# A ring of row blocks for xT, zeroed edge blocks in A, and output stores tile by tile on the sync queue

## The chip, the cores and the metric

The kernel runs on one core of a Trainium2 chip. The metric is device time in microseconds (us); "time" below is that of one whole execution. A profiled execution is described by its span, from the first instruction to the last, and by its own device time, which is a little longer.

## The reference

The input x has 4 images of 256 channels, 64 by 64, in float32. Two layers follow each other.

```python
# layer 0: attention over 49 dilated neighbours, the weights of which are computed from x
k = conv(x, w1 (128,256,7,7), dilation 2, padding 6) + b1
k = conv(k, w2 (49,128,1,1)) + b2
attn = softmax(k, axis=1)                       # 49 shares at each pixel
xp = pad(x, 6)                                  # zeros around the image
shifts = [xp[:, :, 2u:2u+64, 2v:2v+64] for u in 0..6, v in 0..6]
x = einsum('bkchw,bkhw->bchw', shifts, attn)    # each pixel: weighted sum of 49 neighbours
# layer 1: residual bottleneck, batch norm with the batch's own moments
h = relu(bn(conv1x1(x, 256->64)))
h = relu(bn(conv3x3(h, 64->64)))
h = bn(conv1x1(h, 64->256))
return relu(h + x)
```

## The kernel before, in words

Since the dilation is 2, pixels of even and odd rows and columns never mix. The image is therefore handled as four subimages (q = 0 to 3) of 32 by 32 pixels for each of four images: 16 units (b, q), the order of which is in `units`.

**Layer 0, the shares (to about 500 us).** The 7x7 convolution is done along rows by a short-convolution transform on VectorE and along columns by matmuls into eight PSUM banks (`column_convs`, L263), once for each transform point and half of the channels. Then `exponents` and `shares` make the softmax. `shares` writes the 49 shares of a pixel into wide zero-padded rows (`pads`), and `turn` (L556) transposes these rows on TensorE, so that they become `amat`: for each group g of images, column pair c and block m of rows, a matrix A that holds for every output pixel its shares, laid out over the 128 input pixels (4 rows of 32) that it can reach. ScalarE (L574) and VectorE (L572) copy A from PSUM.

**Layer 0, the sum (about 503 to 661 us).** `gather(n, half)` (L728) multiplies, for unit n and half of the channels, tiles of xT (pixels on partitions, channels along the row) by A. There are two xT tiles per unit, c = 0 and c = 1. Tile c = 0 holds the rows of the subimage shifted by 3, c = 1 by 1. A tile has NT + 1 = 9 blocks of 128 pixels; block 0 begins and block 8 ends outside the image, and the parts outside are zeros. In each c, nine matmuls i = 0 to 8 add into one PSUM bank of 512 columns, i = 0 and i = 8 with 64 columns each, the others with 128. The stationary operand is block i of the xT tile, the moving one is A. Everything is float32; each such matmul stands in the profile as two records, each with a weight load of its own.

The tiles for unit n + 2 are brought by `more_xt`, after the gathers of unit n have been issued: `load_xt` (L109) zeroes blocks 0 and 8 on GpSimd (L113, L114) and loads tile c = 0 by three DMAs on the sync queue (L115 the first rows, L116 the main body, L120 the last rows); `shift_xt` (L122) makes tile c = 1 from tile c = 0, its lower 64 partitions by a copy on ScalarE (L124), its upper 64 by a copy on GpSimd (L125) and a memset of the last block (L126). There are two pairs of tiles, so that unit n + 2 uses the pair of unit n. All of them lie in one large tile, `outer`.

`keep_y` copies the sums from PSUM, on VectorE for half 0 (L768) and on ScalarE for half 1 (L766), and stores them to DRAM on the sync queue (L769). After every second unit `conv1` (L780) does the first 1x1 convolution of a finished pair of units and gathers statistics (L788).

**Layer 1.** The first batch norm follows the last `conv1` (L850 to L911). The 3x3 convolution is done partly directly (L947), partly by a transform (L959). The moments of the third convolution's result are worked out from h itself (L1020, L1024) and then in small steps at L1040 to L1053. Finally, for each of 16 output tiles of 128 channels by 2048 pixels, four times: a matmul (`conv3`, L1007), a fused multiply-add of the residual on VectorE (L1065), and a relu on ScalarE (L1069) into one of four tiles `ops`. Each tile is stored by a DMA of 1 MB, issued on ScalarE's queue (L1073).

**What sets the order.** In the blocks `manual_schedule(...)` the order on the named engines is the order of the code. The softmax and `turn` part, up to `more_xt(1)`, is such a block for VectorE, TensorE, ScalarE and the sync queue, not for GpSimd. The gather loop (L799 to L815) and all that follows are in none: there the framework orders each engine's queue when the program is built. [...]

Of the kernel before, what the change touches and what calls it, by code (L numbers as in the profile page):

```python
# [43 lines left out]
AF = mybir.ActivationFunctionType  # L44
ALU = mybir.AluOpType
# [3 lines left out]
P = 128  # L49
B, C, H, W = 4, 256, 64, 64  # L50
# [5 lines left out]
MID = 64  # L56
# [37 lines left out]
def conv_seq_kernel(ctx: ExitStack, tc: tile.TileContext, xp, xt, w1, b1, w2t, b2, m1t, g1, be1,  # L94
# [14 lines left out]
    def load_xt(t, b, q, c=0):  # L109

        src = xt[b].rearrange("j p q c -> (j p) q c")[:, q, :]
        r0 = 2 * c - 3
        nc.gpsimd.memset(t[:, 0, :], 0.0)  # L113
        nc.gpsimd.memset(t[:, NT, :], 0.0)  # L114
        nc.sync.dma_start(out=t[-r0 * R : P, 0, :], in_=src[: (4 + r0) * R])  # L115
        nc.sync.dma_start(  # L116
            out=t[:, 1:NT, :],
            in_=src[(4 + r0) * R : (4 * NT + r0) * R].rearrange("(a p) c -> p a c", p=P),
        )
        nc.sync.dma_start(out=t[: -r0 * R, NT, :], in_=src[(4 * NT + r0) * R :])  # L120

    def shift_xt(t, x):  # L122

        nc.scalar.copy(t[:MID], x[MID:])  # L124
        nc.gpsimd.tensor_copy(t[MID:, :NT], x[:MID, 1:])  # L125
        nc.gpsimd.memset(t[MID:, NT], 0.0)  # L126

# [9 lines left out]
    ut = arena[:, UT:].rearrange("p (h n v) -> p h n v", h=NH, v=KV)  # L139

    amat = arena[:, :AT].rearrange("p (g x c m e) -> p g x c m e", g=2, x=R // 2, c=2, e=4)
    XT = (NT + 1) * C
    xts = {}

    units = [(b + 2 * g, 2 * a + c) for b in range(2) for g in range(2) for c in range(2) for a in range(2)]
# [410 lines left out]
    def turn(s, h, shared=False):  # L556

        row = pads[(2 * s + h) % 3]
        for j in range(4):
            pt = accall[:, 2 * (n_turn[0] % NS) : 2 * (n_turn[0] % NS) + 2].rearrange("p a (m n) -> p (a m) n", n=P)  # L560
            if h == 0 and s == 0:
                pt = accall[:, :2].rearrange("p a (m n) -> p (a m) n", n=P)
            n_turn[0] += 1
            for k in range(2):
                for w in range(4):
                    o = 35 - (WS * s + 4 * h + w) + P * (1 - k)
                    nc.tensor.transpose(pt[:, 4 * k + w, :], row[:, j, w, o : o + P], ident)  # L567
            for g in range(2):
                dst = amat[:, g, 2 * (2 * s + h) + j % 2, j // 2].rearrange("p (k n) e -> p k n e", k=2)
                src = pt[:, :, 64 * g : 64 * g + 64].rearrange("p (k w) n -> p k n w", k=2)  # L570
                if shared and g:
                    nc.vector.tensor_copy(dst, src)  # L572
                else:
                    nc.scalar.copy(dst, src)  # L574
# [49 lines left out]
    for n, (p, factor, left) in enumerate(passes):  # L624
# [8 lines left out]
        for s in range(NS):  # L633
# [12 lines left out]
            if p is None and 0 < s < NS - 1:  # L646
# [2 lines left out]
                exponents(s - 1)  # L649
                shares(s - 1)  # L650

    xtiles = [outer[:, i * XT : (i + 1) * XT].rearrange("p (a c) -> p a c", c=C) for i in range(4)]
# [14 lines left out]
    with tc.manual_schedule(  # L669
        engines={mybir.EngineType.DVE, mybir.EngineType.PE, mybir.EngineType.Activation, mybir.EngineType.SP}  # L670
    ):
        turn(0, 1)
        load_xt(xtiles[0], *units[0])
        exponents(2)
        turn(1, 0)
        exponents(3)
        shares(2)
        turn(1, 1)
        turn(2, 0)
        shares(3)  # L680
        load_xt(xtiles[1], *units[0], 1)
        turn(2, 1, True)
        turn(3, 0, True)
        turn(3, 1, True)
        xts[(*units[0], 0)], xts[(*units[0], 1)] = xtiles[:2]
        nc.scalar.preload_act_table(AF.Sqrt)
        more_xt(1)
# [35 lines left out]
    def bank(kind):  # L723

        n_bank[kind] += 1
        return accall[:, 5 * kind + n_bank[kind] % (5 - 2 * kind)]

    def gather(n, half):  # L728

        b, q = units[n]  # L730
        m = (b // 2 * Q + q) * NT
        pts = []
        for c in range(2):
            x = xts[b, q, c]
            a = amat[:, b % 2, :, c]
            pt = bank(0)
            for i in range(NT + 1):
                lo, hi = max(0, 128 * i - 64), min(1024, 128 * i + 64)
                o = 64 * max(0, i - 1)

                blocks = slice(m + i - 1, m + i + 65, 65)
                if i == 0:
                    blocks = slice(m + 64, m + 65)
                if i == NT:
                    blocks = slice(m + NT - 1, m + NT)
                nc.tensor.matmul(  # L746
                    pt[:, o : o + hi - lo],
                    x[:, i, half * P : (half + 1) * P],
                    a[:, :, blocks, :].rearrange("p x m e -> p m x e"),
                    start=(i == 0),  # L750
                    stop=(i == NT),
                    skip_group_check=True,
                )
            pts.append(pt)
        return pts

    def keep_y(n, half, pts):
# [242 lines left out]
        load_y(n)  # L1000
    sc2, sh2 = from_sums(sums2, bn12[:, 2:3], bn12[:, 3:4])

    def conv3(b, q, i, half):
        a, c = divmod(q, 2)
        part, slot, q = slice(a * MID, (a + 1) * MID), b % 2, b // 2 * 2 + c
        pt = pb_.tile([P, 512], F32, tag="pb", name="pconv3")
        nc.tensor.matmul(  # L1007
            pt, w3m[part, half * P : (half + 1) * P], h2[part, slot, q, 512 * i : 512 * (i + 1)], start=True, stop=True
        )
        return pt  # L1010


    moments = pb_.tile([P, 512], F32, tag="pb", name="moments")
# [20 lines left out]
    one = small(1)[:MID]  # L1034
    mv3 = small(NH, 2)
    sq3 = small(NH, 1)
    nc.gpsimd.memset(one, 1.0)
    for g in range(2):
        half = slice(g * MID, (g + 1) * MID)
        nc.vector.tensor_copy(prod[half], moments[half, half])  # L1040
    nc.vector.tensor_copy(sums, moments[:, P : P + 1])
    pt = pb_.tile([P, 512], F32, tag="pb", name="pprod")
    nc.tensor.matmul(pt[:MID, :C], prod, w3m, start=True, stop=True)
    nc.vector.tensor_tensor(w3p, pt[:MID, :C], w3m[:MID], ALU.mult)
# [1 line left out]
    for half in range(NH):  # L1046
        c = slice(half * P, (half + 1) * P)
        nc.tensor.matmul(pm[:, half, 0:1], w3m[:, c], sums, start=(half == 0), stop=True, skip_group_check=True)
        nc.tensor.matmul(pm[:, half, 1:2], w3p[:, c], one, start=False, stop=True, skip_group_check=True)
    nc.scalar.mul(mv3, pm, 1.0 / (B * H * W))  # L1050
    nc.vector.tensor_tensor(sq3, mv3[:, :, 0:1], mv3[:, :, 0:1], ALU.mult)
    nc.vector.tensor_tensor(mv3[:, :, 1:2], mv3[:, :, 1:2], sq3, ALU.subtract)
    sc3, sh3 = affine(mv3[:, :, 0], mv3[:, :, 1], bn3[:, 0, :], bn3[:, 1, :], NH)  # L1053


    n_out = 0
    for slot in range(2):
        for i in range(2):
            for half in range(NH):
                o = {b: ops[(n_out + n) % 4] for n, b in enumerate((slot, 2 + slot))}  # L1060
                n_out += 2
                for b in (slot, 2 + slot):
                    for q in (0, 2, 1, 3):
                        v = ys[b, q, i][:, half, :]
                        nc.vector.scalar_tensor_tensor(  # L1065
                            v, conv3(b, q, i, half), sc3[:, half : half + 1], v, ALU.mult, ALU.add
                        )
                        dst = o[b].rearrange("p (r a) (w c) -> p a c r w", a=2, c=2)[:, q // 2, q % 2]
                        nc.scalar.activation(  # L1069
                            dst, v.rearrange("p (r w) -> p r w", w=R), AF.Relu, bias=sh3[:, half : half + 1]  # L1070
                        )
                for b in (slot, 2 + slot):
                    nc.scalar.dma_start(  # L1073
                        out=out[b, half * P : (half + 1) * P, 2048 * i : 2048 * (i + 1)],
                        in_=o[b].rearrange("p r w -> p (r w)"),
                    )


def _constants():
# [51 lines left out]
```

## Time and profile before

| what | value |
|---|---|
| median of 3 runs | 813.5 us (808.98 to 813.88) |
| profiled execution, own time | 815.58 us |
| its span | 813.4 us |
| granted TensorE clock, mean | 0.969 |
| TensorE matmuls, weight loads, busy | 741.9 us, 604.4 us |
| VectorE, ScalarE, GpSimd busy | 573.7 us, 300.4 us, 79.3 us |
| DMA | 150.26 MB, mean 185 GB/s |

Own time and span differ by 2.2 us, which lie around the program's own instructions. "PE" is TensorE's matmul row, "PEld" its weight loads, "DVE" VectorE, "ACT" ScalarE, "POOL" GpSimd, "SP" the sync engine; a "q" after an engine's name is its sequencer, which waits and issues DMAs. In a line of groups, "x1152" counts instructions, then come the busy time of the group in us, the mean duration of one in ns, and after the second bar the idle time of the engine just ahead of them with what ended it. In a timeline a line merges neighbouring instructions of a kind: start, length, engine, line, operation, count, and in brackets the idle time before the first. A window's line gives for each engine its busy time and the count in it.

### The profile page before, as it was taken

To read this page: it belongs to the slowest core of one execution; us is meant where nothing else is said; L and a number is where in the kernel's file an instruction comes from. 1 tells how busy PE (TensorE), PEld (TensorE's weight loads), DVE (VectorE), ACT (ScalarE), POOL (GpSimd) and SP (SyncE) were. 2 spreads that over 40 slices of the span, in tenths; PEclk is the share of its full clock that TensorE was granted. 3 is DMA by queue.
4 is the path that set the end of the run, shared out by engine and by line. 5 is a ranking of instruction groups with operands and counts; after the bars stand their busy time and mean duration, and the time that the engine had idled before them with its cause. 6 is when DMAs were issued, how large, how long until landed. Compare 5 with 4: busy or idle time off the path is not lost. (4 is left out here: it accounts for less than half of the span.)

```text
span 813.4 us, 10844 instructions
## 1 busy us (share of the span) xinstructions
PE 741.9 (91%) x4192; PEld 604.4 (74%) x4192; DVE 573.7 (71%) x673; ACT 300.4 (37%) x587; POOL 79.3 (10%) x137
## 2 busy tenths in 40 slices
PE   0949989999999999979999999999999979979993
PEld 0938968888888888858888889887888864439641
DVE  4489989999466999999999866122232337764695
ACT  4640165102541102111111268333444436344497
POOL 3210000001000010000003002222322200000000
PEclk9979998999999999998999999999999999998997
DMA  8931099703798876111110013666766669360298
GB/s 287 363 158 40 3 330 317 328 36 157 256 331 332 326 292 236 49 40 31 49 40 1 3 56 100 207 207 207 230 225 207 207 220 350 129 205 3 104 373 350
DMA packets 58949, 150.26 MB, mean 185 GB/s; under 512 B 7314, under 2 KB 35602, under 8 KB 54546
## 3 DMA queue, kind: packets, MB, share of 16 engines
q1 hardware_dynamic: 48624, 124.34, 43.4%
q10 hardware_dynamic: 10274, 25.23, 8.0%
q8 instruction: 33, 0.54, 0.3%
q14 instruction: 18, 0.15, 0.1%
HBM read 93.81 MB, written 55.74 MB: 184 GB/s over the span
## 5 line engine op out<-in xcount | busy, mean ns | idle before, releaser
L263 PE MATMUL acc<-arena 128*128 128x343 f32 (+3 forms) x2000 | 383.9, 355 | 20.8 <-DVE arena L152 20.6
L263 PEld LDWEIGHTS acc<-arena 128*128 128x128 f32 x2000 | 323.8, 193 | 79.9 <-issue 14.1
L152 DVE SCALAR_TENSOR_TENSOR arena<-arena 128x1024 f32<-128x1024 f32 (+7 forms) x192 | 290.6, 1560 | 28.0 <-PE acc L263 17.3
L746 PEld LDWEIGHTS acc<-arena,outer 128*128 128x128 f32 x1152 | 129.5, 192 | 8.5 <-issue 6.5
L746 PE MATMUL acc<-arena,outer 128*128 128x128 f32 (+1 forms) x1152 | 130.8, 275 | 1.8 <-POOL outer L126 1.8
L788 DVE BATCH_NORM_STATS2 st<-acc 128x6 f32<-128x512 f32 x16 | 11.1, 695 | 73.8 <-PE acc L780 73.7
L287 ACT COPY sv<-acc 128x392 f32<-128x392 f32 x40 | 19.0, 484 | 103.9 <-PE acc L263 101.7
L171 ACT COPY stage<-raw 128x128 f32<-128x128 f32 x128 | 43.7, 417 | 21.9 <-DMA raw<-in_xp_dram 21.5
L326 PE MATMUL acc<-powers,w1raw 128*128 128x196 f32 (+1 forms) x196 | 45.7, 397 | 6.3 <-DMA w1raw<-in_w_dram 4.9
L326 PEld LDWEIGHTS acc<-powers,w1raw 128*128 128x128 f32 x196 | 44.8, 315 | 6.9 <-issue 6.7
L591 ACT COPY outer<-acc 128x784 f32<-128x784 f32 x8 | 6.5, 812 | 101.1 <-PE acc L263 81.2
L124 ACT COPY outer<-outer 64x2304 f32<-64x2304 f32 x15 | 31.7, 2110 | 32.2 <-DMA outer<-in_xt_dram 27.7
L1007 PE MATMUL pconv<-arena,w3m 64*128 64x512 f32 x128 | 41.2, 635 | 0.0
L152 DVE SCALAR_TENSOR_TENSOR outer<-outer 128x784 f32<-128x784 f32 (+2 forms) x47 | 36.9, 839 | 3.6 <-DMA arena<-y_dram 3.6
L768 DVE COPY bks<-acc 128x256 f32<-128x256 f32 x32 | 12.1, 420 | 35.6 <-PE acc L746 35.6
L1007 PEld LDWEIGHTS pconv<-arena,w3m 64*128 64x128 f32 x128 | 19.1, 185 | 20.5 <-DVE arena L1065 15.4
L1069 ACT ACTIVATE outer<-arena 128x512 f32<-128x512 f32 x50 | 32.8, 749 | 3.7 <-DVE arena L844 1.4
L608 ACT COPY acc<-bks 128x392 f32<-128x392 f32 x40 | 18.5, 488 | 42.5 <-DVE outer L593 33.6
L1065 DVE SCALAR_TENSOR_TENSOR arena<-pconv,arena 128x512 f32<-128x512 f32 x50 | 33.3, 744 | 0.0
L125 POOL COPY outer<-outer 64x2048 f32<-64x2048 f32 x15 | 28.3, 1885 | 44.4 <-DMA outer<-in_xt_dram 43.6
L574 ACT COPY arena<-acc 128x512 f32<-128x512 f32 x52 | 27.1, 715 | 14.8 <-PE acc L567 14.4
L959 PE MATMUL pconv<-outer,arena 128*128 128x512 f32 x72 | 31.1, 592 | 0.0
(144 smaller groups left out, 627.4 us busy)
## 6 DMA issues: line engine op xcount, KB each, us to landing
raw<-in_xp_dram SPq DMA_DIRECT2D x36, 608.0 KB, 5.5
out_dram<-outer ACTq DMA_DIRECT2D x16, 1024.0 KB, 4.1
outer<-in_xt_dram SPq DMA_DIRECT2D x17, 896.0 KB, 5.8
arena<-y_dram SPq DMA_DIRECT2D x25, 512.0 KB, 8.6
fsort_dram<-stage SPq DMA_DIRECT2D x2, 4864.0 KB, 15.1
arena<-fsort_dram SPq DMA_DIRECT2D x8, 1216.0 KB, 10.6
y_dram<-outer SPq DMA_DIRECT2D x16, 512.0 KB, 4.7
aside_dram<-sv ACTq DMA_DIRECT2D x40, 196.0 KB, 5.8
```

What stands on the lines that cost most here:

```text
L124: nc.scalar.copy(t[:MID], x[MID:])
L125: nc.gpsimd.tensor_copy(t[MID:, :NT], x[:MID, 1:])
L152: nc.vector.scalar_tensor_tensor(out, in0, scalar, in1, ALU.mult, ALU.add)
L171: (last if last and k + a == 2 else nc.scalar.copy)(d[:, k, :, PLACE[b], 2 * a : 2 * a + 2, i : i + count], raw[:, lo : lo + 4 * count - 3 ...
L263: nc.tensor.matmul(acc[i][d][:, o : o + (hi - lo) * K], xi[:, i, CW * w : CW * w + CW, :].rearrange("p x t -> p (x t)"), u[i][:, lo * K : ...
L326: nc.tensor.matmul(pw[:, o : o + n], w1raw[:, :, u * K7 + v], powers[:, u, :n], start=(u == 0), stop=(u == K7 - 1), skip_group_check=True,)
L574: nc.scalar.copy(dst, src)
L746: nc.tensor.matmul(pt[:, o : o + hi - lo], x[:, i, half * P : (half + 1) * P], a[:, :, blocks, :].rearrange("p x m e -> p m x e"), start=( ...
L959: nc.tensor.matmul(m[k], wu[:, k, j, :], vs[k][:, g, j : j + R, :], start=(j == 0), stop=(j == 1))
L1007: nc.tensor.matmul(pt, w3m[part, half * P : (half + 1) * P], h2[part, slot, q, 512 * i : 512 * (i + 1)], start=True, stop=True)
L1065: nc.vector.scalar_tensor_tensor(v, conv3(b, q, i, half), sc3[:, half : half + 1], v, ALU.mult, ALU.add)
L1069: nc.scalar.activation(dst, v.rearrange("p (r w) -> p r w", w=R), AF.Relu, bias=sh3[:, half : half + 1])
```

## The change

The xT tiles lose their ninth block. The last rows of the image (L120) go into those partitions of block 0 that lie ahead of the first row, so that block 0 holds the first and the last rows at once, and the tile is a ring of eight blocks. The memsets of the tiles go. In `shift_xt`, GpSimd copies seven blocks one place down and then block 0 into the last place.

In `gather`, the matmuls with i = 0 and i = 8, 64 columns each, become one with 128 columns, which uses block 0 for both; it is issued last, after the seven full matmuls of c = 0 and of c = 1. Since block 0 now holds rows that do not belong to one of the two output blocks, A's entries for these are set to 0 by `zero_edges` on GpSimd, 10 memsets after each s of `turn`. A's blocks are laid out interleaved, (n k) for (k n), so that the two that a matmul reads are neighbours.

In the third batch norm the division by the count moves to operands made earlier, and VectorE copies the four moments from PSUM where ScalarE scaled them. The output loop goes tile by tile, stores each tile on the sync queue as soon as it is done, and does the first and the last of the 16 tiles in two halves of 256 columns with a DMA of 512 KB each.

```diff
         r0 = 2 * c - 3
-        nc.gpsimd.memset(t[:, 0, :], 0.0)
-        nc.gpsimd.memset(t[:, NT, :], 0.0)
         nc.sync.dma_start(out=t[-r0 * R : P, 0, :], in_=src[: (4 + r0) * R])
...
-        nc.sync.dma_start(out=t[: -r0 * R, NT, :], in_=src[(4 * NT + r0) * R :])
+        nc.sync.dma_start(out=t[: -r0 * R, 0, :], in_=src[(4 * NT + r0) * R :])
 
     def shift_xt(t, x):
         nc.scalar.copy(t[:MID], x[MID:])
-        nc.gpsimd.tensor_copy(t[MID:, :NT], x[:MID, 1:])
-        nc.gpsimd.memset(t[MID:, NT], 0.0)
+        nc.gpsimd.tensor_copy(t[MID:, : NT - 1], x[:MID, 1:])
+        nc.gpsimd.tensor_copy(t[MID:, NT - 1], x[:MID, 0])
...
-    XT = (NT + 1) * C
+    XT = NT * C
...
-                    o = 35 - (WS * s + 4 * h + w) + P * (1 - k)
+                    o = 35 - (WS * s + 4 * h + w) + P * k
...
-                dst = amat[:, g, 2 * (2 * s + h) + j % 2, j // 2].rearrange("p (k n) e -> p k n e", k=2)
+                dst = amat[:, g, 2 * (2 * s + h) + j % 2, j // 2].rearrange("p (n k) e -> p k n e", k=2)
...
+    def zero_edges(s):
+        for g in range(2):
+            for c, above, below in ((0, ((0, 96),), ((96, P),)), (1, ((0, 32),), ((32, 64), (64, P)))):
+                for block, parts in ((0, above), (2 * NT - 1, below)):
+                    for p0, p1 in parts:
+                        nc.gpsimd.memset(amat[p0:p1, g, 4 * s : 4 * s + 4, c, block :: 2 * NT, :], 0.0)
...
         turn(0, 1)
+        zero_edges(0)
...
         turn(3, 1, True)
+        zero_edges(3)
...
-        m = (b // 2 * Q + q) * NT
...
-            for i in range(NT + 1):
-                lo, hi = max(0, 128 * i - 64), min(1024, 128 * i + 64)
...
+        m = (b // 2 * Q + q) * 2 * NT
+        pts = [bank(0) for c in range(2)]
+        for edge in (False, True):
+            for c in range(2):
+                x = xts[b, q, c]
+                for i in (0,) if edge else range(1, NT):
+                    o = 64 * (i - 1)
+                    blocks = slice(m, m + 2 * NT, 2 * NT - 1) if edge else slice(m + 2 * i - 1, m + 2 * i + 1)
+                    dst = pts[c].rearrange("p (m n) -> p m n", n=64)
+                    nc.tensor.matmul(
+                        dst[:, :: NT - 1] if edge else pts[c][:, o : o + 128],
+                        x[:, i, half * P : (half + 1) * P],
+                        amat[:, b % 2, :, c, blocks, :].rearrange("p x m e -> p m x e"),
+                        start=(i == 1), stop=edge, skip_group_check=True,
+                    )
...
-    nc.gpsimd.memset(one, 1.0)
+    nc.gpsimd.memset(one, 1.0 / (B * H * W))
...
-    nc.vector.tensor_copy(sums, moments[:, P : P + 1])
+    nc.vector.tensor_scalar(sums, moments[:, P : P + 1], 1.0 / (B * H * W), None, ALU.mult)
...
-    nc.scalar.mul(mv3, pm, 1.0 / (B * H * W))
+    nc.vector.tensor_copy(mv3, pm)
...
+    blocks = [(slot + 2 * g, i, half) for slot in range(2) for i in range(2) for half in range(NH) for g in range(2)]
+    for k, (b, i, half) in enumerate(blocks):
+        o = ops[k % 4]
+        n = 256 if k in (0, len(blocks) - 1) else 512
+        for lo in range(0, 512, n):
+            for q in (0, 2, 1, 3):
+                v = ys[b, q, i][:, half, lo : lo + n]
+                nc.vector.scalar_tensor_tensor(
+                    v, conv3(b, q, i, half, lo, n), sc3[:, half : half + 1], v, ALU.mult, ALU.add
+                )
+                rows = slice(lo // 16, (lo + n) // 16)
+                dst = o[:, rows].rearrange("p (r a) (w c) -> p a c r w", a=2, c=2)[:, q // 2, q % 2]
+                nc.scalar.activation(dst, v.rearrange("p (r w) -> p r w", w=R), AF.Relu, bias=sh3[:, half : half + 1])
+            first = 2048 * i + 4 * lo
+            nc.sync.dma_start(
+                out=out[b, half * P : (half + 1) * P, first : first + 4 * n],
+                in_=o[:, rows].rearrange("p r w -> p (r w)"),
+            )
```

More of the change, by code (lines that the diff above doesn't have):

```diff
@@ L678, in conv_seq_kernel @@
         turn(1, 1)
+        zero_edges(1)
         turn(2, 0)
@@ L682, in conv_seq_kernel @@
         turn(2, 1, True)
+        zero_edges(2)
         turn(3, 0, True)
         turn(3, 1, True)
+        zero_edges(3)
         xts[(*units[0], 0)], xts[(*units[0], 1)] = xtiles[:2]
@@ L730, in gather @@
         b, q = units[n]
-        m = (b // 2 * Q + q) * NT
[L732 to L736, printed above, removed]
-            for i in range(NT + 1):
-                lo, hi = max(0, 128 * i - 64), min(1024, 128 * i + 64)
[L739 to L754, printed above, removed]
+        m = (b // 2 * Q + q) * 2 * NT
[11 more added lines that the diff above has]
+                        amat[:, b % 2, :, c, blocks, :].rearrange("p x m e -> p m x e"),
+                        start=(i == 1),
+                        stop=edge,
+                        skip_group_check=True,
+                    )
         return pts
@@ L1001, in conv_seq_kernel, with conv3 @@
     sc2, sh2 = from_sums(sums2, bn12[:, 2:3], bn12[:, 3:4])
-    def conv3(b, q, i, half):
+    def conv3(b, q, i, half, lo, n):
         a, c = divmod(q, 2)
@@ L1006, in conv3 @@
         pt = pb_.tile([P, 512], F32, tag="pb", name="pconv3")
+        lo += 512 * i
         nc.tensor.matmul(
-            pt, w3m[part, half * P : (half + 1) * P], h2[part, slot, q, 512 * i : 512 * (i + 1)], start=True, stop=True
+            pt[:, :n], w3m[part, half * P : (half + 1) * P], h2[part, slot, q, lo : lo + n], start=True, stop=True
         )
-        return pt
+        return pt[:, :n]
     moments = pb_.tile([P, 512], F32, tag="pb", name="moments")
@@ L1053, in conv_seq_kernel @@
     sc3, sh3 = affine(mv3[:, :, 0], mv3[:, :, 1], bn3[:, 0, :], bn3[:, 1, :], NH)
[L1056 to L1076, printed above, removed]
+    blocks = [(slot + 2 * g, i, half) for slot in range(2) for i in range(2) for half in range(NH) for g in range(2)]
[16 more added lines that the diff above has]
+            )
 def _constants():
```

## The prediction

> **What bounds the kernel now.** I read the page's busy times first, then the groups by shape, then tables by window of the two stages that change, then timelines at their seams.
>
> ```profile
> PE 741.9 (91%) x4192; PEld 604.4 (74%) x4192; DVE 573.7 (71%) x673; ACT 300.4 (37%) x587; POOL 79.3 (10%) x137
> ...
> L746 PEld LDWEIGHTS acc<-arena,outer 128*128 128x128 f32 x1152 | 129.5, 192 | 8.5 <-issue 6.5 <-POOL outer L126 2.0
> L746 PE MATMUL acc<-arena,outer 128*128 128x128 f32 x896 | 113.9, 279 | 0.0
> L746 PE MATMUL acc<-arena,outer 128*128 128x64 f32 x256 | 37.8, 264 | 1.8 <-POOL outer L126 1.8
> ```
>
> The gather stage has 1152 records of TensorE: 16 units x 2 halves x 2 c x 9 matmuls x 2. A fifth (256) have 64 columns. Whether these cost half or the same as the others decides what merging them is worth.
>
> ```profile
> 512.00:521.00 9.00, 9.00 (x83) 9.00 (x82) 1.51 (x4) 3.38 (x6) 2.76 (x4) 1.00 0.78 257
> 640.00:660.00 20.00, 20.00 (x164) 17.41 (x163) 5.62 (x12) 7.96 (x14) 4.07 (x4) 1.00 0.50 176
> ...
> 568.87 16.29 PE L746 MATMUL acc<-arena,outer 128*128 128x64 f32 x144
> ...
> 496.26 7.21 PE L567 MATMUL acc<-ident,outer 128*128 128x128 f32 x64
> ```
>
> The columns are length, then busy time of PE, PEld, DVE, ACT, POOL, clock, DMA share, GB/s. In a stretch of gathers alone the weight loads are busy all 9.00 us; VectorE, ScalarE, GpSimd and the DMAs are not. 144 records last 16.29 us; less some 0.2 us for the tail of the last one that is 111.7 ns each, narrow ones among them. 64 transposes, every one of 128 columns, come to (7.21 - 0.2) / 64 = 109.5 ns. So a narrow record costs a full weight load.
>
> The tile loads run close behind:
>
> ```profile
> 552.32 0.38 SPq L120 DMA_DIRECT2D outer<-in_xt_dram  x1
> ...
> 560.95 2.11 ACT L124 COPY outer<-outer 64x2304 f32<-64x2304 f32 x1 [3.06 <-DMA outer<-in_xt_dram]
> ...
> 563.16 2.19 PE L746 MATMUL acc<-arena,outer 128*128 128x64 f32 x18 [1.84 <-POOL outer L126]
> ```
>
> Once, TensorE waits 1.84 us for a c = 1 tile, whose copies started when a load landed 8.6 us after its issue. It is the stage's only such wait.
>
> In the output stage three resources run at nearly the same pace:
>
> ```profile
> 794.00:798.00 4.00, 4.00 (x14) 1.81 (x13) 4.00 (x7) 3.53 (x7) 0.00 (x0) 1.00 0.89 367
> ...
> L1073 ACTq DMA_DIRECT2D out_dram<-outer x16: 338/339/350, 766.2 to 808.6; - x16
> ...
> 806.58 2.00 ACT L1069 ACTIVATE outer<-arena 128x512 f32<-128x512 f32 x3
> 808.60 0.34 ACTq L1073 DMA_DIRECT2D out_dram<-outer  x1
> ```
>
> VectorE is full: 64 operations at 0.66 us (14 in 9.30 us) end at 804.9. ScalarE also issues the stores, at 0.34 us each; it falls behind and ends at 808.6, 3.7 us after VectorE. The last 1 MB then takes 3.9 us to land (the DMA view's range is 3.9 to 5.9) and the span ends at 813.4.
>
> [...]
>
> **The change part by part.**
>
> *Gather.* Per c one matmul, two records, goes: 16 x 2 x 2 x 2 = 128 records. The columns streamed stay the same, 1024 per c. 128 x 111.7 ns = 14.3 us less, on the bound engine. The edge matmul reads A at two places and writes two column groups of one bank; no row shows that. Reads already jump every four elements, so I take 0, at most 20 ns on 128 records = 2.6 us, and no gain below 0, since the weight load floors it.
>
> *Copies out of PSUM.* Both c now finish at the end of a gather, where c = 0 was done 2.0 us before. That is covered by the next gather (32 x 111.7 ns = 3.57 us), except after the last: there `conv1` waits for four L766 copies instead of two. Two take 0.65 us, four 0.65 + 2 x 0.27 = 1.2; +0.5 us.
>
> *Tile loads.* Let E be the end of gather(n, 1), n even. Before, the main load L116 goes 2 us after that gather's start (568.87 to 570.95), L120 at E + 1.4, behind the store of y, and tile c = 1 of unit n + 2 is needed at E + 4.0 + 4.0 + 2.0 = 10.0. After: the main load waits only for the full matmuls of c = 0 (1.6 us after the start, E - 2.0). The loads of block 0 wait for the edge matmul of c = 0, at E - 0.2. Queued behind them on SP: the second y store, which nobody waits for soon. Need: E + 3.57 + 3.57 + 14 x 0.1117 = 8.7. The main load lands after a median 5.8 us, hence E + 4; block 0's pieces (median 4.5 and 1.8) by E + 4.8. The copy on ScalarE is 2.11 us for 2304 columns, about 1.9 for 2048, GpSimd's two (1.89 for 2048 together, a few tenths for the second start) much the same: done at E + 6.8. Slack 1.9 us: hidden. For odd n a `conv1` (3.6 us) lies between too. Bounds: the wait of 1.84 us goes, or such waits come at all seven even units (first rival). I leave it in.
>
> *GpSimd.* 49 memsets leave (15.2 us busy), 40 small ones come at 0.1 to 0.2 us (116 ns for 21 elements, 212 for 144): about 6. Only `zero_edges`(3) is near the path: A's last copies end at 504.1 on ScalarE, the first edge matmul is due 28 records after 503.3, at 506.4. Five memsets at 0.2 us end by 505.1; behind a 1.9 us copy still in time. Cost 0. If it had no cover: at most 2 us, once.
>
> *A's layout.* Copies L574 (0.59 us) and L572 (0.69) write runs of four elements. L766 writes such runs at 370 to 375 ns for 256 elements, a contiguous L711 takes 389. I take 0; at 50 ns on each of 64 copies it is 3 us, and there is no gain to be had.
>
> *Third batch norm.* L1050 (0.17 us, ScalarE) becomes a VectorE copy (L853 is 0.16). The scale moves onto L1041, same length. 0 us, at most 0.1 either way.
>
> *Output.* ScalarE loses 16 issues and follows VectorE. VectorE gains eight operations: one of 512 is 0.66 us, [...](estimate from L768: 256 in 0.38), so one of 256 is 0.39, and each halved tile costs 8 x 0.39 - 4 x 0.66 = +0.5. VectorE ends at 804.9 + 1.0 = 805.9, ScalarE 0.5 later, at 806.4. Last store: 512 KB; a 512 KB store by SP lands after 2.6 us at best, 3.4 (L769 from `bks`) in the median. 1 MB per 2.64 us is 397 GB/s, what the DMAs reach here, so about 0.5 us of backlog: landed 809.9, and 0.9 us to the end as now: 810.8. That is 2.5 us less. Bounds: 0.5 (stores wait for bandwidth) and 3.5.
>
> Sum: -14.3 + 0.5 - 2.5 = -16.3 us. The profiled execution's span goes from 813.4 to 797.1, its own time from 815.6 to 799.3. That execution lies 2.1 us above the median of the runs, 813.5, so the forecast for the median is 797.2.
>
> **Rivals.**
>
> *A: as summed*, 797.2 us. For it: weight loads at 100%, everything else at half load or less.
>
> *B: ScalarE's order eats the gather's gain.* ScalarE's queue has no hand-written order here. Before, at the even units, L124 stands behind the first two L766 copies of gather(n + 1, 1) (537.43 and 537.96, for one). Those copies now come at that gather's end. If L124 stays behind all four, it starts 1.1 us after that end and is done at 3.0, needed at 1.56: TensorE stands 1.4 us at seven units = 10 us, leaving 813.5 - 6.3 = 807.2. Against it: tiles now land before that gather ends, so L124 should be queued ahead.
>
> *C: slower.* Block 0 is freed last. If its first load is queued ahead of the main one, the main load goes at E + 0.5, and L120 behind the y store at E + 1.9. Landing as late as the one above, 8.6 us, and copied in 1.9, the tile is ready at E + 12.4, 3.7 late; seven times that is 25.9: 813.5 - 16.3 + 25.9 = 823.1. It decides from a delay of 16.3 / 7 = 2.3 us per even unit, that is from a landing after E + 9.1. Against it: at the median landing, 4.5, nothing is late.
>
> **Chances and numbers.** A measurement here tells about 1%, 8 us, from no change. A 0.70, its own range 794 to 802. B 0.20, of which a quarter (stalls below 1.2 us) is still over 1% faster. C 0.10. Hence faster by over 1% 0.75, within 1% 0.15, slower 0.10. Low end: the 1.84 us wait gone and 3.5 us at the output give 794.4, rounded to 793; high end: into B, 808.5; C is left out.
>
> **What would show it.** 1024 records at L746's successor, spaced 111.7 ns, and about 143 us from the first gather to the last `conv1` where it is 158; PE waits there below 3 us. Wrong if the spacing exceeds 115 ns, or if PE waits for the shift copies (B) or for the tile loads (C) at unit after unit. At the end: no DMA issue in ScalarE's queue, ScalarE within 1 us of VectorE, and under 5 us from VectorE's last operation to the end of the span (8.5 now).

## The result, and the profile after

| | before | after |
|---|---|---|
| median of the runs | 813.07 us (4 runs) | 800.27 us (4 runs, 799.13 to 802.33) |
| ratio after / before, 95% interval | | 0.9865 [0.9831, 0.9900] |
| profiled execution: own time, span | 815.58, 813.4 us | 799.53, 797.6 us |
| first gather starts | 503.30 us | 499.12 us |
| first gather to the last `conv1`'s first matmul | 158.13 us | 148.44 us |
| last `conv1` | 3.65 us | 3.92 us |
| from its end to VectorE's first output operation | 97.52 us | 97.24 us |
| VectorE's first output operation to the end | 50.83 us | 48.87 us |

The change is faster by 1.35% (1.0 to 1.7). The forecast was 797.2 us for the median and 797.1 for the span. The median fell by 12.8 us where 16.3 was forecast. The span of 797.6 agrees almost to the digit, but that is luck: two misses cancel in it. The spans differ by 15.8 us, of which 4.2 arose ahead of the first gather, where the forecast had nothing. The gathers gave 9.7 where 13.8 was forecast, and the output 1.95 where 2.5 was.

The page's busy times after:

```profile
PE 729.1 (91%) x4080; PEld 590.2 (74%) x4080; DVE 574.6 (72%) x682; ACT 297.7 (37%) x594; POOL 75.7 (9%) x143
```

The groups by shape after. The gather's matmul is now at L752, the memsets of `zero_edges` at L657, the shift copy on ScalarE at L123.

```profile
L752 PE MATMUL acc<-arena,outer 128*128 128x128 f32 x1024 | 118.8, 277 | 3.1 <-issue 2.9 <-POOL arena L715 0.2
L752 PEld LDWEIGHTS acc<-arena,outer 128*128 128x128 f32 x1024 | 116.0, 193 | 11.3 <-issue 10.1 <-ACT arena L771 0.8 <-POOL arena L715 0.4
...
L123 ACT COPY outer<-outer 64x2048 f32<-64x2048 f32 x15 | 28.4, 1895 | 38.4 <-DMA outer<-in_xt_dram 38.4
...
L657 POOL MEMSET arena<- 32x128 f32 x24 | 4.7, 197 | 1.0
```

1024 records have taken the place of 1152, and their weight loads fell from 129.5 to 116.0 us: 13.5 us of busy time, near the forecast gain of 14.3. But PE's idle time ahead of L752 rose from 1.8 to 3.1 us, put down to "issue", which names nobody. The timeline of TensorE says where it lies:

```profile
520.73 12.55 PE L752 MATMUL acc<-arena,outer 128*128 128x128 f32 x110
533.51 2.25 PE L752 MATMUL acc<-arena,outer 128*128 128x128 f32 x18 [0.23 <-issue]
...
610.42 2.87 PE L752 MATMUL acc<-arena,outer 128*128 128x128 f32 x18 [1.92 <-issue]
613.22 1.12 PE L785 MATMUL acc<-outer,w1m 128*64 128x512 f32 x1
```

110 records run without a break: 32 + 32 + 32 + 14. The fifteenth record of the fourth gather is the first to read tile c = 1, and there TensorE waits. The bracket understates it, since a matmul's end is modelled. By starts of records, 510 ns passed at 533.5 where 112 is the rule. The same happened at 552.1 (532 ns), 570.6 (471), 610.4 (2199) and 630.9 (806): 3.96 us over the rule. Each is the tile of an even unit. Who was late is seen in the timelines of the sync queue and of ScalarE at the first of these. L114 is the main load, L113 and L119 are the first and last rows, which go into block 0, and L774 is the store of y.

```profile
522.62 0.38 SPq L114 DMA_DIRECT2D outer<-in_xt_dram  x1
523.10 2.89 SPq L774 DMA_DIRECT2D y_dram<-outer  x2
526.08 0.44 SPq L113 DMA_DIRECT2D outer<-in_xt_dram  x1
526.61 0.39 SPq L119 DMA_DIRECT2D outer<-in_xt_dram  x1
...
531.52 1.90 ACT L123 COPY outer<-outer 64x2048 f32<-64x2048 f32 x1 [5.89 <-DMA outer<-in_xt_dram]
```

gather(n, 1) ended at E = 524.4. Two stores of y stand between the main load and block 0's loads, and the second of them waits for `keep_y`'s four copies, until E + 1.2. So block 0's loads, which could have gone at E, go at E + 1.7 and E + 2.2 and land at E + 6.9 and E + 7.0. The copy starts at once, ends at E + 9.0, and TensorE wanted the tile at E + 8.7.

The wait of 1.92 us costs a second time. A table by window (length, busy time of PE, PEld, DVE, ACT, POOL, then clock, DMA share, GB/s):

```profile
600.00:609.00 9.00, 8.50 (x77) 8.31 (x75) 1.42 (x4) 1.38 (x4) 2.07 (x2) 1.00 0.89 302
609.00:618.00 9.00, 7.58 (x35) 4.13 (x36) 1.56 (x4) 3.38 (x7) 2.07 (x2) 0.81 0.41 146
```

After it the granted clock is 0.81 on average over the window. The `conv1` matmul at 613.22, shown above, takes 1.12 us where it has 0.64 after the other waits. From the wait's end to the next gather 7.38 us pass, where 5.76 do after the wait at 533.51: 1.6 us lost.

At the end, the timelines of the three engines of the output (VectorE L1070, ScalarE L1075, sync queue L1077):

```profile
786.82 5.19 DVE L1070 SCALAR_TENSOR_TENSOR arena<-pconv,arena 128x512 f32<-128x512 f32 x11
...
787.65 5.28 ACT L1075 ACTIVATE outer<-arena 128x512 f32<-128x512 f32 x11
...
784.49 8.80 SPq L1077 DMA_DIRECT2D out_dram<-outer  x5
```

VectorE ends at 792.0, ScalarE at 792.9 (3.7 us behind VectorE before), and the last store is issued at 792.96. The span ends 4.6 us later. In these last microseconds the DMAs are the limit, with the second half-tile store behind the first:

```profile
790.00:792.00 2.00, 0.00 (x0) 0.00 (x0) 2.00 (x6) 2.00 (x6) 0.00 (x0) 0.50 0.97 397
792.00:794.00 2.00, 0.00 (x0) 0.00 (x0) 0.01 (x1) 0.94 (x3) 0.00 (x0) 0.50 0.96 389
```

### The profile page after: what moved, and what is told of

It reads as the page before. It is cut to its first block, busy times and chain, and to the rows that moved or that the text cites. A ratio compares the mean times of both kernels' runs of the same rounds, so it can differ in the third digit from the quotient of the medians.

```text
span 797.6 us, 10675 instructions
## 1 busy us (share of the span) xinstructions
PE 729.1 (91%) x4080; PEld 590.2 (74%) x4080; DVE 574.6 (72%) x682; ACT 297.7 (37%) x594; POOL 75.7 (9%) x143
## 4 chain that ended last, share of the span: by engine, by line
PE 72%; DVE 15%; ACT 5%; DMA 4%; issue 2%; POOL 0%; SPq 0%; ACTq 0%; DVEq 0%; POOLq 0%
PE acc L262 42%; PE acc L752 13%; DVE arena L151 9%; PE acc L785 4%; PE pconv L964 3%; PE pdirect L952 3%; DVE arena L1070 3%; PE acc L566 2%; PE moments L1030 2%; PE acc L325 2%; ACT outer L1075 1%; DMA outer<-in_xt_dram 1%; ACT arena L573 1%; DMA w1raw<-in_w_dram 1%; PE pturn L1026 1%
## 5 line engine op out<-in xcount | busy, mean ns | idle before, releaser
L752 PEld LDWEIGHTS acc<-arena,outer 128*128 128x128 f32 x1024 | 116.0, 193 | 11.3 <-issue 10.1
L752 PE MATMUL acc<-arena,outer 128*128 128x128 f32 x1024 | 118.8, 277 | 3.1 <-issue 2.9
L1013 PE MATMUL pconv<-arena,w3m 64*128 64x512 f32 (+1 forms) x144 | 43.0, 587 | 0.6 <-DVE arena L1070 0.6
L123 ACT COPY outer<-outer 64x2048 f32<-64x2048 f32 x15 | 28.4, 1895 | 38.4 <-DMA outer<-in_xt_dram 38.4
L1013 PEld LDWEIGHTS pconv<-arena,w3m 64*128 64x128 f32 x144 | 20.7, 185 | 21.9 <-DVE arena L1070 16.0
L1075 ACT ACTIVATE outer<-arena 128x512 f32<-128x512 f32 (+1 forms) x58 | 34.7, 695 | 1.3 <-DVE arena L849 1.1
L1070 DVE SCALAR_TENSOR_TENSOR arena<-pconv,arena 128x512 f32<-128x512 f32 (+1 forms) x58 | 34.3, 667 | 0.0
L124 POOL COPY outer<-outer 64x1792 f32<-64x1792 f32 x15 | 25.1, 1676 | 95.5 <-DMA outer<-in_xt_dram 80.1
L573 ACT COPY arena<-acc 128x512 f32<-128x512 f32 x52 | 27.1, 708 | 14.8 <-PE acc L566 14.4
```

What stands on the lines that cost most here:

```text
L752: nc.tensor.matmul(dst[:, :: NT - 1] if edge else pts[c][:, o : o + 128], x[:, i, half * P : (half + 1) * P], amat[:, b % 2, :, c, blocks, ...
L1013: nc.tensor.matmul(pt[:, :n], w3m[part, half * P : (half + 1) * P], h2[part, slot, q, lo : lo + n], start=True, stop=True)
L1070: nc.vector.scalar_tensor_tensor(v, conv3(b, q, i, half, lo, n), sc3[:, half : half + 1], v, ALU.mult, ALU.add)
L1075: nc.scalar.activation(dst, v.rearrange("p (r w) -> p r w", w=R), AF.Relu, bias=sh3[:, half : half + 1])
```

## The experiments

"Stage" is here the time from the first gather to the end of the last `conv1`. "Output" is the time from VectorE's first output operation to the end of the span. Both are read from the profiled execution. Ratios are to the kernel before, run in the same set. The medians are of 4 or 5 runs, of 20 for e4 and of 2 for e8.

| kernel | median us | ratio [95%] | stage us | output us |
|---|---|---|---|---|
| before | 813.07; 810.74; 811.87 in three sets | 1 | 161.78 | 50.83 |
| after | 800.27 | 0.9865 [0.9831, 0.9900] | 152.36 | 48.87 |
| e1_load_first | 795.98 | 0.9815 [0.9788, 0.9842] | 145.67 | 49.46 |
| e2_edge_in_place | 799.46 | 0.9851 [0.9815, 0.9888] | 150.67 | 48.88 |
| e3_ring_only | 804.23 | 0.9912 [0.9881, 0.9942] | 153.24 | 50.88 |
| e4_output_only | 808.12 | 0.9973 [0.9959, 0.9987] | 161.88 | 48.78 |
| e5_first_whole | 795.58 | 0.9796 [0.9767, 0.9824] | 146.99 | 47.98 |
| e6_first_whole_edge | 795.99 | 0.9799 [0.9759, 0.9839] | 145.89 | 48.01 |
| e7_act_stores | 800.30 | 0.9853 [0.9832, 0.9874] | 152.66 | 48.80 |
| e8_no_last_block | 799.88 | 0.9852 [0.9818, 0.9887] | 148.92 | 50.81 |

### e1_load_first: the loads ahead of the second store of y

The theory: the order of the sync queue makes the tiles late. The rivals: the release of block 0 by the edge matmul, which is issued last, or DMAs that are short of bandwidth in this stage.

```diff
-        keep_y(n, 1, gather(n, 1))
+        pts = gather(n, 1)
         if n + 2 < len(units):
-            more_xt(n + 2)
+            load_xt(xtiles[2 * (n % 2)], *units[n + 2])
+        keep_y(n, 1, pts)
+        if n + 2 < len(units):
+            more_xt(n + 2, False)      # shift_xt only
```

> The changed kernel, with the three loads of a tile written ahead of the copies and the store of y of gather(n, 1), so that on the sync queue block 0's two loads stand ahead of the second y store and not behind it. Theory Q (queue order): in the changed kernel TensorE waits 0.4 to 2.1 us at five even units (4.0 us in all, plus about 1.6 us of records at half clock after the longest) because block 0's loads sit behind that store and land 7 us after the end of gather(n, 1). Here they should land about 4.8 us after it, the waits should be gone, the stage from the first gather to the last conv1 should take about 147 us where it takes 152, and the whole 796 us where the changed kernel takes 800. Rival R (late release): it is the edge matmul, placed last, that frees block 0 too late; then the waits stay at 2 us or more and the whole is 799 to 801. Rival D (the DMAs are short of bandwidth in this stage): the waits stay too.

The same seam in the timelines of TensorE and the sync queue of e1 (the store of y is L775, the gather L753):

```profile
523.02 14.56 PE L753 MATMUL acc<-arena,outer 128*128 128x128 f32 x128
...
524.91 0.39 SPq L114 DMA_DIRECT2D outer<-in_xt_dram  x1
525.40 0.51 SPq L775 DMA_DIRECT2D y_dram<-outer  x1
526.66 0.33 SPq L113 DMA_DIRECT2D outer<-in_xt_dram  x1
527.08 0.46 SPq L119 DMA_DIRECT2D outer<-in_xt_dram  x1
527.94 0.41 SPq L775 DMA_DIRECT2D y_dram<-outer  x1
```

128 records now run through. Block 0's loads go at E and E + 0.4 (E = 526.7), land by E + 6.1, and the copy is done at E + 8.1, 0.6 us before the need. Over the stage two waits are left (258 and 599 ns between records), 0.6 us over the rule in all, and the clock stays full. The stage fell by 6.7 us. A comparison of the two traces, record by record, puts this at the seams between units: 0.40, 0.42, 0.36, 1.60 and 0.69 us at the five waits and 0.07 behind each, 1.55 at the halved clock, and 1.3 at unit 10. There the main load of the change itself goes behind the second store and lands at E + 8.0, and `conv1` stands between the gathers in three pieces of 2, 4 and 10 records, where e1 has it in one. How the 1.3 us divides between the late tile and the pieces no run shows; the kernel before loses 1.1 us at unit 10 with `conv1` in two pieces and no late tile. So the order of the loads and stores on the sync queue was the cause of most of what was missing. It was not the bandwidth: e1 moves the same bytes, and all but 0.6 us of the waits are gone. The landings expected at E + 4.8 were not reached.

### e2_edge_in_place: the edge matmul directly after its seven full ones

```diff
-        for edge in (False, True):
-            for c in range(2):
+        for c in range(2):
+            for edge in (False, True):
```

> The changed kernel, with the edge matmul of each c right after its seven full ones, so that block 0 of tile c = 0 is free 1.8 us earlier and the copies out of PSUM of c = 0 start 1.8 us earlier. Most of the block 0 loads still stand behind a y store in the sync queue. Theory Q: the second y store can leave about 0.6 us earlier, so the tile is complete about 0.6 us earlier and the small waits (0.4 to 0.7 us) go, the long one may stay: 798 to 799 us. Rival R (late release): all waits go: 796 us. Rival D: no change, 800 us.

Block 0 of tile c = 0 comes free 1.6 us earlier, so the first load of it goes at E - 1.6 at some units, but the last one still goes at E + 1.3 to E + 2.5, behind the second store. The waits stay at five seams (472, 280, 443, 1764 and 902 ns between records), although the theory had the small ones go, and a sixth of 1.17 us stands ahead of unit 10, for its main load. The stage of 150.67 is 1.7 us below the change's, about what the clock gives, which this time did not drop after the longest wait (it is 1.00 over the 9 us from 609). The ratio lies within the change's interval. So an earlier release alone does not take the waits away. Since the last load stands behind the store in e2 as well, whether it would help with the loads ahead is left to e6.

### e3_ring_only and e4_output_only: the two halves of the change

e3 has the ring, `zero_edges` and the merged matmul, with the third batch norm and the output of before. e4 is the reverse.

e3 against the change:

```diff
-    nc.vector.tensor_copy(mv3, pm)
+    nc.scalar.mul(mv3, pm, 1.0 / (B * H * W))
...
-    for k, (b, i, half) in enumerate(blocks):
...
-            nc.sync.dma_start(
+    for slot in range(2):
...
+                for b in (slot, 2 + slot):
+                    nc.scalar.dma_start(
```

> The changed kernel with the third batch norm and the output loop of the kernel before. The ring's part alone: the traces of before and after differ by 9.4 us from the first gather to the first direct convolution, so 813.1 - 9.4 = 803.7 us. If a part of the 12.8 us was chance of the run ahead of the gathers, the two parts add up to about 11.6; if the parts help each other, this one is below 802 or above 806.

e4 against the kernel before:

```diff
-    nc.scalar.mul(mv3, pm, 1.0 / (B * H * W))
+    nc.vector.tensor_copy(mv3, pm)
...
-                for b in (slot, 2 + slot):
-                    nc.scalar.dma_start(
...
+    for k, (b, i, half) in enumerate(blocks):
...
+            nc.sync.dma_start(
```

> The kernel before with the third batch norm and the output loop of the changed one. By the two traces the part from the first direct convolution to the end is 2.2 us shorter (142.1 to 139.9), so 813.1 - 2.2 = 810.9 us; my prediction had 2.5. The rival, that the stores are bound by the rate of the DMAs and nothing is gained by who issues them, says 812.6 or more.

e3 saves 6.5 us of its set's 810.74, where the expectation, as a saving, had 9.4; the interval reaches from 4.7 to 9.6. e4 saves 2.6 us, where 2.2 was expected. Their sum, 9.1 us, is somewhat below the 11 us of the ratio of the whole, within the intervals. e3's stage shows the same waits as the change (566, 586, 560, 2240 and 1116 ns), and e4's stage is that of before. In e4 the output takes 48.78 us, in e3 50.88: 2.0 us for the output part, as between before and after. Nothing here shows that the parts help or disturb each other.

### e5_first_whole and e6_first_whole_edge: e1 with whole output tiles, and with e2's order

```diff
-        n = 256 if k in (0, len(blocks) - 1) else 512
+        n = 512
```

> The kernel of e1_load_first with every output tile done whole: 64 operations on VectorE, 16 stores of 1 MB, none in halves. Theory (the halves cost what they save): VectorE ends 1.0 us earlier, counted from the first direct matmul of the 3x3 convolution, because 2 x 0.5 us of extra operations go; the last store is 1 MB in place of 512 KB and, with the rate of 397 GB/s, lands 1.3 us later after its issue, so the stretch from that matmul to the end stays at 139.8 us within 0.4 us and the median at 796 us. Rival (the halves pay, since the last half is all that stands behind VectorE's end): the stretch grows to 140.5 us or more. In both the gather stage stays at about 145.7 us.

> e5_first_whole with the edge matmul of each c issued directly after the seven full ones of the same c, so that block 0 of tile c = 0 comes free 1.8 us earlier. Theory (the order of the sync queue was the cause, and the time of release was not): with the loads already ahead of the store nearly nothing is left to gain; the gather stage is 145 us, within 1 us of that of e1_load_first (145.7), and the median within 1.5 us of e5. Rival (the late release of block 0 counts as well): the two waits of TensorE left in e1_load_first, 0.15 and 0.49 us, go, and the clock stays full: the stage falls to 144 us or less.

The stretch from the first direct matmul to the end was 138.54 us in e5 and 139.46 in e6, which have the same code there. So it scatters by 0.9 us and can't decide what the halves are worth. The narrower output time can: 47.98 and 48.01 us with whole tiles, 48.78 to 49.46 in the five kernels with halves. VectorE's part of it is 42.29 and 43.29 us. So both expectations on the halves missed: they cost VectorE the 1.0 us, and give back almost nothing. From the issue of the last store to the end 4.8 us pass with 1 MB, and 4.3 to 5.2 with 512 KB, with the half before still on its way (in the change it lands at 794.96, 2.0 us after the last issue). The timelines of e5's end (VectorE L1074, sync queue L1081):

```profile
785.76 3.38 DVE L1074 SCALAR_TENSOR_TENSOR arena<-pconv,arena 128x512 f32<-128x512 f32 x5
...
787.38 2.96 SPq L1081 DMA_DIRECT2D out_dram<-outer  x2
```

VectorE ends at 789.1, the span at 794.8. The medians of e1, e5 and e6 (795.98, 795.58, 795.99) can't be told apart by these runs. e6's stage, 145.89, shows no gain from an earlier release, as its theory had it, so the late release is not the cause: two waits are left in it as well, 0.85 and 0.29 us over the rule. e5's stage is 1.3 us longer than e1's: three waits hold 1.9 us over the rule in it (1006, 647 and 571 ns), where e1 has 0.6, with the same code up to there. So this much is scatter of the landings. All three kernels beat the one before. Against the change they are ahead by their ratios, 0.980 to 0.982 where it has 0.987, but the intervals of e1 and e6 just touch that of the change; the stages, 5 to 7 us shorter, say the same.

### e7_act_stores: the output stores on ScalarE again

```diff
-            nc.sync.dma_start(
+            nc.scalar.dma_start(
```

> The changed kernel with its 18 output stores issued by ScalarE in place of the sync engine, tiles in halves as in the change. Theory (the part of the output that pays is ScalarE freed from issuing): ScalarE again pays 18 x 0.34 = 6 us, falls behind VectorE, ends 3 to 4 us after it where it is 0.9 now, and the stretch from the first direct matmul to the end grows from 139.9 to about 142.5 us, the median from 800 to some 802.5. Rival (the gain comes from stores of half a tile and the order by tiles, not from the queue): the stretch stays within 0.5 us of 139.9 us.

The theory fell. ScalarE ends at 794.0, 1.15 us after VectorE where it was 0.93, and the output takes 48.80 us (48.87 in the change). 18 issues of 0.34 us cost nothing that can be seen. The timeline of ScalarE and its queue in e7 shows why:

```profile
785.81 2.07 ACT L1075 ACTIVATE outer<-arena 128x512 f32<-128x512 f32 x3
787.78 0.76 ACT L1075 ACTIVATE outer<-outer,arena 128x512 f32<-128x512 f32 x1
787.91 0.34 ACTq L1077 DMA_DIRECT2D out_dram<-outer  x1
788.44 2.48 ACT L1075 ACTIVATE outer<-arena 128x512 f32<-128x512 f32 x4
```

A tile's last relu ends at 787.88, the first relu of the next tile is already running (787.78 to 788.54), and the store is issued beside it. The kernel before, whose code has two stores after each pair of tiles, shows the other case:

```profile
800.95 2.00 ACT L1069 ACTIVATE outer<-arena 128x512 f32<-128x512 f32 x3
802.98 0.34 ACTq L1073 DMA_DIRECT2D out_dram<-outer  x1
803.42 0.76 ACT L1069 ACTIVATE outer<-outer,arena 128x512 f32<-128x512 f32 x1 [0.47 <-ACT outer L1069]
```

There the pair's second store stands directly behind the relu that it waits for and ahead of the next one, and ScalarE stands 0.47 us. That occurs at seven seams, 3.3 of the 3.7 us by which ScalarE was late; the pair's first store, issued beside a running relu, costs nothing. So with the order by tiles, where each store stands one relu behind its tile, the move to the sync queue adds nothing, and the halves, by e5 and e6, do not pay either. What is left as the gain is that ScalarE no longer stands at the seams. The order by tiles is enough for that; whether the move to the sync queue with the order by pairs would have been enough too, no run shows.

### e8_no_last_block: the price of a narrow record

The kernel before with the ninth matmul of each c left out of the gathers; the sums of the output blocks it fed are incomplete.

```diff
-            for i in range(NT + 1):
+            for i in range(NT):
```

> The kernel before, with the ninth matmul (i = 8, 64 columns) of every c in the gathers left out, so the last two rows' worth of sums is incomplete: 1024 records in place of 1152, and nothing else moved (tiles, loads, copies and layout as before). It prices a narrow record by itself. Theory (a narrow record costs a full weight load, 111.7 ns): the gather stage falls from 161.8 us by 128 x 111.7 ns = 14.3 us to about 147.5 us. Rival (it costs about half, 59 ns): it falls by 7.6 us to about 154.2 us. If tile loads or copies fall behind the faster TensorE in the kernel before as well, waits longer than 1 us appear between gathers and the spacing of records inside them stays at 111.7 ns.

The groups by shape and TensorE's timeline of e8:

```profile
L746 PEld LDWEIGHTS acc<-arena,outer 128*128 128x128 f32 x1024 | 116.4, 194 | 8.6 <-issue 5.7 <-DMA outer<-in_xt_dram 2.9
```

```profile
591.00 4.99 PE L746 MATMUL acc<-arena,outer 128*128 128x128 f32 x30 [2.71 <-DMA outer<-in_xt_dram]
```

The stage fell by 12.86 us. Waits hold 3.14 us of what is left (2988 and 373 ns between records), where before they held 2.01. Without the waits the gain is 14.0 us, or 109 ns for each of 128 records: a whole weight load. This leaves out two losses that nearly cancel: 1.2 us at half clock behind the wait in e8, and 1.1 us before, at unit 10. Two units without either take 19.80 us before and 18.07 in e8: 1.73 us for 16 records, 108 ns each. The rival's half price, 59 ns, is out. The faster TensorE meets only one late tile in e8. But the loads did not stay as they were: no matmul reads the last block any more, so the load of the last rows goes at E - 0.8 or earlier at five of the seven even units, where before it goes at E + 1.3. So e8 can't tell whether the pace alone would make tiles late. An estimate from the trace of before says that it nearly would: there tile c = 1 was ready at E + 8.6 to E + 9.2 (once at E + 12.1), in time for a need at E + 10.0, but at or just behind the E + 8.7 of the faster gathers.

## Why the prediction was right or wrong

The total was in range, and the price of a record, on which most of it rests, was right. The order of the tile loads was not, and in the profiled span 4.2 us that are not the change's made up for it.

*Gather.* Right. The price of 111.7 ns shows in the spacing of the 1024 records, and e8 gives 108 to 109 ns by itself. The edge matmul's two places cost nothing visible: 128 records in e1 take 14.56 us, 112 ns each once the last one's tail is off. Without late tiles (e1) the stage is 16.1 us shorter than before. 13.8 for the records at 108 ns, 2.1 for the wait of before, which the forecast had left in, and 1.1 for its `conv1` in two pieces at unit 10, which the forecast did not see, less 0.6 of waits left and 0.3 for the last `conv1`, make 16.1.

*Tile loads.* This step failed, in its order. It had "Queued behind them on SP: the second y store, which nobody waits for soon", but the second store is queued ahead of them. It waits for `keep_y`'s copies, and block 0's loads wait behind it: gone at E + 1.7 and E + 2.2 in place of E - 0.2. The landing was too hopeful as well. I took medians of 4.5 and 1.8 us, "by E + 4.8"; with the order that I had assumed, e1 lands them at E + 5.1 to E + 7.1 at the even units. In the change block 0's loads land at 531.27 and 531.45, 0.17 and 0.35 us after the store ahead of them, at 531.10; in e1 at 532.65 and 532.83, 0.18 and 0.36 us after the first store, at 532.47. At all five late tiles of the change the last load landed 0.35 to 0.54 us behind the store in front of it, 4.8 to 6.5 us after its own issue. The slack of 1.9 us was 1.6 to -0.4 us in e1 and 0.2 to -2.0 in the change. So TensorE waits 4.0 us, where the text allowed 3, and the halved clock (1.55 us) and unit 10 (1.3) come on top. The stretch that the text put at about 143 us takes 148.4; it is 141.7 in e1. With this, a sign that the prediction had named for being wrong came true: TensorE waits for the tile loads at five of the seven even units. At 4.0 us in all the waits were too short to take the total out of its range.

*Copies out of PSUM.* Forecast +0.5 us ahead of the last `conv1`; measured +0.27 in its own length. In e2 and e6, where c = 0 finishes early again, it is back at the 3.65 us of before. Covered elsewhere, as forecast.

*GpSimd, A's layout, third batch norm.* Free, as forecast. The 40 memsets take 197 to 213 ns on average, depending on their shape, 8.1 us where I had about 6. L573's copies of A take 708 ns on average in the new layout against 715 of L574 before, and the copy that replaces L1050 takes 161 ns. From the last `conv1` to the first output operation the two kernels differ by 0.3 us.

*Output.* The size was near, the reason only in part. VectorE's +1.0 us is exact (42.28 to 43.29 us for all output operations). ScalarE ended 0.93 us behind it, not 0.5, and the end came 4.63 us after the last issue, not 4.4. That makes -1.95 in place of -2.5. "ScalarE loses 16 issues and follows VectorE" holds for the second half alone: by e7 the time of the issues was not what held ScalarE, but the 0.47 us that it stood at seven of them. The halves, which the forecast counted on for a shorter last store, gave back next to nothing (e5, e6). From VectorE's end to the end of the span 5.6 us passed; the text had said under 5.

*The 4.2 us ahead of the gathers.* Not forecast, and not the change's. Up to there the ten kernels differ only in memsets, a few small loads and the layout of A, and their first gather starts anywhere from 499.1 to 503.4 us, without order: 503.30 and 502.95 with the old tiles, 501.30 in e8, 503.43 in e2, 499.12 in the change. Most of it is the granted clock early on. Windows of the kernel before:

```profile
118.00:124.00 6.00, 2.89 (x11) 2.37 (x10) 5.93 (x3) 4.36 (x13) 0.00 (x0) 0.78 0.93 285
124.00:129.00 5.00, 5.00 (x14) 3.41 (x14) 4.97 (x4) 2.52 (x9) 0.00 (x0) 0.59 0.91 308
```

and of the change, at the same work one microsecond earlier:

```profile
117.00:123.00 6.00, 2.97 (x15) 2.28 (x14) 5.93 (x3) 3.32 (x10) 0.00 (x0) 1.00 0.99 361
123.00:128.00 5.00, 5.00 (x23) 3.83 (x22) 4.97 (x3) 2.77 (x9) 0.00 (x0) 1.00 0.99 315
```

Clock 0.78 and 0.59 against 1.00. Record by record, the change is 0.45 us ahead of the kernel before when these windows begin and 3.48 us ahead when they end, so they hold 3.0 of the 4.2 us. This is not the change's either: e7 keeps the full clock there as the change does, but e5 and e6, with the same code up to there, run the same 6.8 us at half clock as the kernel before (there from 121.3 to 128.2 us); e5's first gather starts at 503.06 us.

*The rivals.* B and C both foresaw late tiles at even units. B put it on ScalarE's order; in the change ScalarE's copy L123 starts about 0.1 us after the last landing at every even unit (0.07 us at the first one shown), so it was not that. C named the sync queue and a landing after E + 9.1 as the point from which the change loses. The landings were E + 6.5 to E + 8.7: its mechanism in mild form, in another order (the main load first in most units, the stores between).

## What to carry to other kernels

When a change frees a buffer later or splits a load in pieces, write down the queue of the issuing engine in full, with every store in it and what that store waits for: here a load that was free to go stood for 1.7 us behind a store that waited for copies, and 6.7 us that the fewer matmuls had earned came to light only when the load went first. Price a landing by what stands ahead of it in its queue, and not by the median of that transfer: a load of 32 KB, with a median of 1.8 us in the kernel before, took 5.2 us at the first late tile and landed 0.17 us behind the store ahead of it. And ask of an instruction that an engine issues for DMA not how long it is, but whether it must wait for the operation directly ahead of it on the same engine: directly behind it the store cost 0.47 us, one operation later nothing that could be seen.

## What the runs showed of the hardware

In four kernels TensorE's clock fell to half after a wait of about 2 us or more. After idle times of 1.92 us (the change), 1.97 (e3), 2.12 (e7) and 2.71 (e8) a window of 9 us that starts within the wait shows a clock of 0.81. After 1.84 us (before, at 563.2) and after e2's longest wait (1.49 us) a window of 9 us that holds the wait shows 1.00. The change around its wait, which ends at 610.42, and then the window of before:

```profile
608.45:611.86 3.41, 1.49 (x14) 1.47 (x14) 0.00 (x0) 2.94 (x5) 0.39 (x1) 1.00 0.73 242
611.86:615.27 3.41, 3.41 (x14) 1.90 (x14) 0.00 (x0) 0.00 (x0) 2.07 (x2) 0.50 0.51 184
615.27:618.68 3.41, 3.41 (x19) 1.44 (x16) 2.21 (x5) 1.66 (x2) 0.00 (x0) 1.00 0.00 0
...
561.00:570.00 9.00, 7.16 (x47) 4.46 (x47) 2.54 (x6) 5.13 (x6) 4.25 (x4) 1.00 0.43 143
```

In the change the clock fell 1.44 us after TensorE had gone on, and was back 3.41 us later. What decides between the 1.84 us of before and the 1.92 us of the change, no run shows.

An issue of 0.34 us on ScalarE's queue ran beside ScalarE's arithmetic at no visible cost in e7 (output 48.80 us, against 48.87 in the change), and stalled it for 0.47 us in the kernel before, where it waited for the operation just ahead.
